# Binding side work to a place in each engine's queue, forming the setups' bias vectors another way, and another end for the last tile, in a four-layer graph network

## The chip, the cores and the metric

The kernel runs on one core of one Trainium2 chip. The metric is the device time of a run in microseconds (us). A core has a matrix engine (TensorE, PE in the profile), three engines for elementwise work (VectorE or DVE, ScalarE or ACT, GpSimd or POOL), and SyncE (SP), which here only issues DMAs. Each engine takes its instructions in the order of its own queue. PE reads its operands in SBUF and writes to PSUM; DVE and ACT read both; DMAs move data between DRAM and SBUF.

## The reference

128 graphs of 64 nodes with 512 features (8192 tokens, fp32) go through four layers. In each, `h = relu(layernorm(x))`, and then `x = x + layer(h)`:

```python
# layer 0 (Wqk gives q and k; the softmax runs over a graph's nodes)
agg = adj @ (k * mask);  w = mask * sum(q * agg, -1) / sqrt(512)
L0 = softmax(w, axis=1)[:, :, None] * (h @ Wv)
# layer 1
weight = adj * exp((h @ Wq.T + bq) @ (h @ Wk.T + bk).T)
L1 = (weight / weight.sum(2)) @ (h @ Wv.T + bv)
# layer 2: eight heads of 64, scores times 2*adj, softmax, then Wo and bo
# layer 3
Xw = h @ Wv + bv;  e = leaky_relu(Xw @ aw[:512] + (Xw @ aw[512:]).T + ab)
A = adj * exp(e);  A = A / A.sum(-1)
L3 = relu(h @ Wk[0] + bk[0] + A @ h @ Wk[1] + bk[1] + A @ A @ h @ Wk[2] + bk[2])
```

Layer 1's scores are formed without q and k: with `M = Wk Wq` folded once, `h_i M h_j + u . h_i + c . h_j + d` is the score, where u comes from Wq and bk, c from Wk and bq, and d = bq . bk. Layer 3's Xw is likewise never formed: `aw` is multiplied into Wv once (two vectors of 512, and two scalars from bv).

## The kernel before

**Tiling.** A block is 256 tokens (two tiles of 128, four graphs); there are 32 blocks. Layers 0 and 1 run over the blocks in pairs (`steps`: layer 0 of blocks b and b+1, then layer 1 of both), write x to DRAM, then layer 2 runs over all blocks, then layer 3. Each step holds `norm` (statistics on DVE, `rstd` on POOL at L171, `h` on ACT at L178), `transposed` (PE L189; the two halves of hT are copied out by DVE, L194, and ACT, L192), and products with 512x512 weights.

**Products.** The class `Product` multiplies 256x512 by 512x512 in seven products of half the size instead of eight (Strassen and Winograd's scheme). On the data side it needs the sums S1 to S4, which `sums` makes on POOL from hT (L213 to L216, S1 first, S3 last); on the weight's side it needs T1 to T4, four POOL instructions of 128x512 for each weight (L87, or L98 where they are postponed). Product 1 needs only hT, product 5 needs S1. The seven products are issued in three stages: `first` (L263), `second`, and `late`; `side_by_side` (L341) puts the stages of two products beside each other and runs the steps of other work, handed in as `between`, in the gaps. `keep_ab` (L275) copies partial results out of PSUM: p1 by ACT (L277), u2 by DVE (L278). `add_to` (L331) adds layer 2's output product to x.

**Postponed weight sums.** `later` puts a weight's four sums in a list, and `chore` (L95) takes a number from it. It is called between the stages of the steps. A scheduler decides where on POOL they go: it orders the instructions of each engine by when their operands are there, and may put them ahead of instructions that were written earlier. `tc.issue_after(i)` exists in the framework: instructions inside it are put behind instruction i on their engine, with no data passed and no wait added between engines.

**Start and setups.** L131 to L143 issue the first loads: x and adjT on SP, Wq's four parts on ACT's queue, Wk's four on SP, L0_Wv, then mcol (the node mask, L142) and the bias columns. `setup0` folds layer 0's weights and forms `msc` (L437) from mcol; layer 0 multiplies with it at L504 (agg) and forms the per-graph softmax (wd L511, sm_w L394, mn L522, att, x L538). `transpose_weight` writes a weight's transpose over the weight (PE L410, copies L414 on ACT and L416 on DVE). `folded` makes M (PE L424). `setup1` does the same for layer 1, and takes u, c and d from 24 matmuls: u (pu1, L453) from 16 of one column, c (pc1) from four of 128x512, whose stationary operand is bq laid out 128 times, and d (pd1, L468). In layer 1 the dot product with c is DVE's `hc` (L556). `setup3` multiplies Wv by the two columns of aw: for each, a column laid out 128 times is stationary (awr), and four 128x512 matmuls (pu, L740) give the vector on all partitions; pc (L751) does the scalars. It runs at layer 2's block 28.

**Layer 2** adds its output bias L2_bo to x on POOL (L977) at the start of each block. **The last tile** of layer 3 (`layer3_end`, L855) goes from PSUM through ACT (tz, L860), POOL (L862) and DVE (L863) to the output DMA.

Of the kernel before, what the change touches and what calls it, by code (L numbers as in the profile page):

```python
# [8 lines left out]
FP = mybir.dt.float32  # L9
# [16 lines left out]
def kernel(ctx: ExitStack, tc: tile.TileContext, a: dict, out: bass.AP):  # L26
# [68 lines left out]
    def chore(n: int = 1):  # L95
        for _ in range(min(n, len(chores))):
            w, (to, x, y) = chores.pop(0)
            nc.gpsimd.tensor_tensor(w[:, to], w[:, x], w[:, y], ALU.subtract)  # L98
# [36 lines left out]
    first = load_x(0, x_d[rows(0), :], 0), load_adjT(0, 0)  # L135
    f0 = [
# [4 lines left out]
    mcol = const.tile([P, n_tok // P], FP, tag="mcol", name="mcol")  # L141
    nc.sync.dma_start(mcol, a["maskcol"])  # L142
    b1q, b1k, b2q, b2k = (column(n) for n in ("L1_bq", "L1_bk", "L2_bq", "L2_bk"))  # L143
# [56 lines left out]

    def sums(hT, name: str, places=("S", "S")):
# [14 lines left out]
        nc.gpsimd.tensor_tensor(S3, A11, A21, ALU.subtract)  # L216
# [3 lines left out]
    class Product:  # L220
# [40 lines left out]
        def first(self, ops, w, beside: bool = False):  # L261

            self.early(ops, w, (1, 5) if beside else (1, 6))  # L263
            if not beside:
                self.keep_ab()
# [7 lines left out]
        def keep_ab(self):  # L273
# [4 lines left out]
            nc.vector.tensor_tensor(self.u2, self.b, self.p1, ALU.add)  # L278
# [51 lines left out]
        def add_to(self, x):  # L330
# [8 lines left out]
            nc.gpsimd.tensor_tensor(x[:, 1, F:], self.u3, x[:, 1, F:], ALU.add)  # L339

    def side_by_side(*parts, between=()):  # L341
# [18 lines left out]
        for acts in between:  # L360
            for act in acts:
                act()

# [76 lines left out]
    def setup1():  # L440


        qT, kT = (factor(a[f"L1_W{c}"], c, 1, nc.sync) for c in "qk")
        w1v = fetched("L1_Wv", 3, nc.sync)
        yield
        for w, c in zip((qT, kT), "qk"):
# [3 lines left out]
        pu = ps_sc.tile([P, K], FP, tag="sc", name="pu1")  # L450
        for i in range(K):
            for k in range(K):
                nc.tensor.matmul(  # L453
                    pu[:, i : i + 1], qT[:, k, i * P : (i + 1) * P], b1k[:, k : k + 1],
                    start=(k == 0), stop=(k == K - 1),
                )
        u = const.tile([P, K], FP, tag="u1", name="u1")
        nc.vector.tensor_copy(u, pu)
        bqr = med.tile([P, K, P], FP, tag="pT", name="bqr", bufs=3)
        nc.vector.tensor_copy(bqr, b1q.unsqueeze(2).to_broadcast([P, K, P]))  # L460
        pc = ps_mm.tile([P, D], FP, tag="mm", name="pc1")
        for k in range(K):
# [619 lines left out]
```

## Time and profile before

| | |
|---|---|
| median of three runs | 2736.61 us (2732.79 to 2737.43) |
| the profiled execution | 2732.14 us, its span 2730.2 us |
| PE busy | 2667.7 us (98%) |
| DVE busy | 1704.9 us (62%) |
| ACT busy | 945.8 us (35%) |
| POOL busy | 1291.3 us (47%) |
| DMA | 128.49 MB, mean 47 GB/s |

The span goes from the first to the last instruction; 1.94 us of the execution lie around it. The page has each engine's busy time, the span in 40 slices of some 68 us with tenths of busy time, the chain of work that ended last, and groups of like instructions. The trace answers further: which instruction an engine waited for and how long, single instructions in a stretch of time, and busy time in chosen windows. A line there names the program line (L248), the engine, the operation, and the tiles (out<-in); a number in square brackets is idle time of the engine just before it and what ended it. Two PE records stand for one fp32 matmul.

### The profile page before, as it was taken

Reading aid. Unit: us, or ns where it says so; the run is one execution under the profiler, and the core shown is the slowest. Engines: PE = TensorE matmul, PEld = TensorE weight load, DVE = VectorE, ACT = ScalarE, POOL = GpSimd, SP = SyncE. Lnnn points to the kernel's source line nnn. Section 1 sums busy time; section 2 is a strip of 40 time slices with the busy share of each in tenths; the row PEclk is TensorE's granted clock in tenths of the full one; section 3 lists DMA queues with packets and bytes.
Section 4 is the critical chain, followed back from the end, with each engine's and each line's share of the span. In section 5 each row is a group of like instructions: output and inputs, shape, how many; then the busy total and the mean of one; then the engine's idle time right before and its main releaser. Section 6 shows DMA issues by size and latency. Waiting matters only on the chain.

```text
span 2730.2 us, 52850 instructions
## 1 busy us (share of the span) xinstructions
PE 2667.7 (98%) x20808; PEld 2263.4 (83%) x20808; DVE 1704.9 (62%) x4386; ACT 945.8 (35%) x2292; POOL 1291.3 (47%) x1586
## 2 busy tenths in 40 slices
PE   8999999999999998999999999999999999999998
PEld 5788888888888887899999989999887777777776
DVE  3566666666666667555555555555567666666664
ACT  2333333433333332333333333333333333333332
POOL 3434343333334337456456456456454455554454
PEclk9999999999999999999999999999999999999999
DMA  4111100111111112111111111111111111111110
GB/s 144 49 39 44 34 34 34 34 35 42 42 34 46 37 44 94 37 36 38 52 36 38 51 36 38 51 37 37 48 64 50 50 51 55 55 55 50 50 49 32
DMA packets 102345, 128.49 MB, mean 47 GB/s; under 512 B 40528, under 2 KB 49744, under 8 KB 102096
## 3 DMA queue, kind: packets, MB, share of 16 engines
q1 hardware_dynamic: 101520, 124.07, 13.6%
q8 instruction: 163, 2.67, 0.4%
q10 hardware_dynamic: 576, 1.05, 0.1%
q14 instruction: 86, 0.70, 0.1%
HBM read 74.76 MB, written 50.33 MB: 46 GB/s over the span
## 4 chain that ended last, share of the span: by engine, by line
PE 71%; DVE 17%; POOL 4%; DMA 4%; ACT 2%; issue 2%; SPq 0%; ACTq 0%; POOLq 0%; DVEq 0%
PE ab_y L248 10%; PE dc_y L248 8%; PE ab_v L248 7%; PE dc_v L248 6%; PE ab_q L241 4%; PE ab_g L248 4%; PE ab_k L241 4%; PE ab_g L241 3%; PE po L386 3%; PE dc_k L241 3%; PE dc_q L241 3%; PE dc_g L248 2%; PE tr L189 2%; DMA x<-x 2%; PE dc_g L241 2%; DVE e L654 2%
## 5 line engine op out<-in xcount | busy, mean ns | idle before, releaser
L178 ACT ACTIVATE h<-x,nmr,rstd 128x512 f32<-128x512 f32 x256 | 198.0, 808 | 223.5 <-DVE nmr L173 188.9
L166 DVE BATCH_NORM_STATS2 stats<-x 128x6 f32<-128x512 f32 x256 | 166.1, 676 | 71.8 <-DMA x<-x 67.5
L171 POOL TENSOR_TENSOR rstd<-ve,neghalf 128x2 f32<-128x2 f32 x128 | 89.7, 700 | 254.6 <-DVE ve L169 254.4
L248 PE MATMUL ab_y<-L_Wk,hT 128*128 128x256 f32 x768 | 204.3, 388 | 3.3 <-DVE u_y L300 2.6
L248 PE MATMUL ab_v<-L_Wv,hT 128*128 128x256 f32 x768 | 201.9, 385 | 3.8 <-DVE u_v L278 2.9
L248 PE MATMUL dc_y<-L_Wk,S 128*128 128x256 f32 x768 | 199.8, 383 | 0.7
L248 PE MATMUL dc_v<-L_Wv,S 128*128 128x256 f32 x768 | 197.2, 379 | 1.7 <-DVE v L302 1.7
L248 PE MATMUL ab_y<-L_Wk,S 128*128 128x256 f32 x768 | 197.8, 380 | 0.0
L248 PE MATMUL ab_v<-L_Wv,S 128*128 128x256 f32 x768 | 197.1, 379 | 0.0
L248 PEld LDWEIGHTS ab_y<-L_Wk,hT 128*128 128x128 f32 x768 | 137.8, 190 | 70.1 <-issue 25.2
L248 PEld LDWEIGHTS dc_y<-L_Wk,S 128*128 128x128 f32 x768 | 144.6, 191 | 26.4 <-DVE y L850 6.9
L248 PEld LDWEIGHTS dc_v<-L_Wv,S 128*128 128x128 f32 x768 | 145.8, 190 | 21.9 <-DVE v L302 2.1
L248 PEld LDWEIGHTS ab_v<-L_Wv,S 128*128 128x128 f32 x768 | 146.1, 190 | 20.0
L862 POOL TENSOR_TENSOR tz<-tz,y 128x512 f32<-128x512 f32 x64 | 92.9, 1452 | 145.8 <-ACT tz L860 145.8
L248 PEld LDWEIGHTS ab_y<-L_Wk,S 128*128 128x128 f32 x768 | 143.8, 191 | 18.3
L248 PEld LDWEIGHTS ab_v<-L_Wv,hT 128*128 128x128 f32 x768 | 133.9, 191 | 19.1 <-DVE u_v L278 3.2
L323 POOL TENSOR_TENSOR qk<-u_q,p_q 128x256 f32<-128x256 f32 x32 | 23.3, 727 | 265.4 <-DVE u_q L307 265.4
L189 PE MATMUL tr<-ident,h 128*128 128x128 f32 x1024 | 135.8, 275 | 3.9 <-ACT h L178 2.2
L189 PEld LDWEIGHTS tr<-ident,h 128*128 128x128 f32 x1024 | 119.9, 142 | 15.7 <-ACT h L178 2.6
L278 DVE TENSOR_TENSOR u_v<-ab_v,p_v 128x256 f32<-128x256 f32 x96 | 40.6, 423 | 126.2 <-ACT p_v L277 126.2
L213 POOL TENSOR_TENSOR S<-hT 128x256 f32<-128x256 f32 x128 | 99.4, 776 | 35.5 <-ACT hT L192 33.1
L216 POOL TENSOR_TENSOR S<-hT 128x256 f32<-128x256 f32 x128 | 106.9, 835 | 1.6 <-DVE hT L194 0.4
(243 smaller groups left out, 6535.8 us busy)
## 6 DMA issues: line engine op xcount, KB each, us to landing
x<-x SPq DMA_DIRECT2D x128, 512.0 KB, 3.4
x<-in_x_dram SPq DMA_DIRECT2D x32, 512.0 KB, 3.5
out_dram<-x SPq DMA_DIRECT2D x31, 512.0 KB, 2.7
adjT<-in_adjT_dram SPq DMA_DIRECT2D x64, 64.0 KB, 2.0
adjq<-in_adj_dram SPq DMA_DIRECT2D x64, 64.0 KB, 2.3
L_Wk<-in_L_Wk_dram SPq DMA_DIRECT2D x16, 256.0 KB, 4.4
L_Wv<-in_L_Wv_dram SPq DMA_DIRECT2D x12, 256.0 KB, 4.6
q<-in_L_Wqk_dram ACTq DMA_DIRECT2D x4, 256.0 KB, 5.9
```

The lines of the kernel that those rows point to most:

```text
L166: nc.vector.bn_stats(stats[:, t, :], x[:, t, :])
L171: nc.gpsimd.tensor_tensor(rstd, ve, neghalf, ALU.pow)
L178: nc.scalar.activation(h, x[:, t, :], AF.Relu, bias=nmr[:, t : t + 1], scale=rstd[:, t : t + 1])
L189: nc.tensor.transpose(pt[:, k, :], h[:, k * P : (k + 1) * P], ident)
L213: nc.gpsimd.tensor_tensor(S1, A21, A22, ALU.add)
L216: nc.gpsimd.tensor_tensor(S3, A11, A21, ALU.subtract)
L241: nc.tensor.matmul(dst[:, m * P : (m + 1) * P], w[:, place, k, m * P : (m + 1) * P], left[:, k, :], start=key not in self.begun, stop=last ...
L248: nc.tensor.matmul(dst, left[:, k, :], w[:, place, k, :], start=key not in self.begun, stop=last and k == 1, skip_group_check=True,)
L278: nc.vector.tensor_tensor(self.u2, self.b, self.p1, ALU.add)
L386: nc.tensor.matmul(ps[t][half[g ^ t]], e[half[g], t, :], us[t][half[g]], start=True, stop=True)
L654: nc.vector.tensor_tensor(eh, eh, mx.unsqueeze(2).to_broadcast([P, TT * hq, N]), ALU.subtract)
L862: nc.gpsimd.tensor_tensor(tz[t], tz[t], y0[:, t, :], ALU.add)
```

## The change

It has seven parts.

- The load of mcol moves to the third place on SP, behind x and adjT.
- `setup1` no longer uses PE for u, c and d. L1_bq and L1_bk are loaded to all 128 partitions, and nine DVE instructions of 128x512 multiply and sum (`accum_out`): four for u, four for c, one for d. c is written to DRAM as a row of 512 and loaded back to all partitions.
- The postponed weight sums, layer 3's bias sums and layer 2's L2_bo additions are issued behind `behind[0]`, which is the last S3 of `sums` or the last POOL addition of `add_to`; in layer 2 at most one sum comes in a block, two at some places.
- `hc` is issued behind `u2` of the value product (`kept`).
- Where two products run side by side, `first` issues product 5 ahead of product 1.
- `setup3` makes aw's two columns stationary: four matmuls of 2x512 and four of 2x1. The result (2x513) goes to DRAM and back to all partitions.
- In the last block, tile 0 is finished by one DVE instruction from PSUM in place of ACT's scaling and POOL's addition.

```diff
@@ -93,9 +93,10 @@
         chores.extend((w, s) for s in sums_of_weights)
     def chore(n: int = 1):
-        for _ in range(min(n, len(chores))):
-            w, (to, x, y) = chores.pop(0)
-            nc.gpsimd.tensor_tensor(w[:, to], w[:, x], w[:, y], ALU.subtract)
+        with tc.issue_after(behind[0].ins):
+            for _ in range(min(n, len(chores))):
+                w, (to, x, y) = chores.pop(0)
+                nc.gpsimd.tensor_tensor(w[:, to], w[:, x], w[:, y], ALU.subtract)
     def fetched(name: str, place: int, queue):
         w = slot(place, name)
@@ -133,14 +134,14 @@
         return w
     first = load_x(0, x_d[rows(0), :], 0), load_adjT(0, 0)
+    mcol = const.tile([P, n_tok // P], FP, tag="mcol", name="mcol")
+    nc.sync.dma_start(mcol, a["maskcol"])
     f0 = [
         factor(a["L0_Wqk"][:, i * D : (i + 1) * D], c, 0, queue)
         for i, (c, queue) in enumerate((("q", nc.scalar), ("k", nc.sync)))
     ]
     w0v = fetched("L0_Wv", 1, nc.sync)
-    mcol = const.tile([P, n_tok // P], FP, tag="mcol", name="mcol")
-    nc.sync.dma_start(mcol, a["maskcol"])
-    b1q, b1k, b2q, b2k = (column(n) for n in ("L1_bq", "L1_bk", "L2_bq", "L2_bk"))
+    b2q, b2k = (column(n) for n in ("L2_bq", "L2_bk"))
     b1v = row("L1_bv")
@@ -213,7 +216,7 @@
         nc.gpsimd.tensor_tensor(S1, A21, A22, ALU.add)
         nc.gpsimd.tensor_tensor(S2, S1, A11, ALU.subtract)
         nc.gpsimd.tensor_tensor(S4, A12, S2, ALU.subtract)
-        nc.gpsimd.tensor_tensor(S3, A11, A21, ALU.subtract)
+        behind[0] = nc.gpsimd.tensor_tensor(S3, A11, A21, ALU.subtract)
         return {1: (A11, B11), 4: (A22, T4), 5: (S1, T1), 6: (S2, T2),
                 2: (A12, B21), 3: (S4, B22), 7: (S3, T3)}
@@ -260,7 +263,7 @@
         def first(self, ops, w, beside: bool = False):
-            self.early(ops, w, (1, 5) if beside else (1, 6))
+            self.early(ops, w, (5, 1) if beside else (1, 6))
             if not beside:
                 self.keep_ab()
@@ -275,7 +278,7 @@
             self.p1, self.u2 = self.temp("p1"), self.temp("u2")
             nc.scalar.copy(self.p1, self.a)
-            nc.vector.tensor_tensor(self.u2, self.b, self.p1, ALU.add)
+            self.kept = nc.vector.tensor_tensor(self.u2, self.b, self.p1, ALU.add)
         def keep_dc(self, bias=None):
@@ -336,7 +339,9 @@
             nc.vector.tensor_tensor(x[:, 0, F:], self.c, x[:, 0, F:], ALU.add)
             nc.vector.tensor_tensor(x[:, 0, :F], self.a, x[:, 0, :F], ALU.add)
             nc.vector.tensor_tensor(x[:, 1, :F], self.d, x[:, 1, :F], ALU.add)
-            nc.gpsimd.tensor_tensor(x[:, 1, F:], self.u3, x[:, 1, F:], ALU.add)
+            behind[0] = nc.gpsimd.tensor_tensor(
+                x[:, 1, F:], self.u3, x[:, 1, F:], ALU.add
+            )
     def side_by_side(*parts, between=()):
@@ -441,40 +447,41 @@
         qT, kT = (factor(a[f"L1_W{c}"], c, 1, nc.sync) for c in "qk")
+
+        bias = big.tile([P, 2, P, K], FP, tag="v", name="b1qk")
+        for i, n in enumerate(("L1_bq", "L1_bk")):
+            nc.sync.dma_start(
+                bias[:, i], a[n].rearrange("(o p) k -> o p k", o=1).to_broadcast([P, P, K])
+            )
         w1v = fetched("L1_Wv", 3, nc.sync)
         yield
+        u = const.tile([P, K], FP, tag="u1", name="u1")
+        cc = small.tile([P, K], FP, tag="cc", name="c1", bufs=1)
+        d = const.tile([P, 1], FP, tag="d1", name="d1")
+        for to, x, by in (
+            *((u[:, k : k + 1], qT[:, k, :], 1) for k in range(K)),
+            *((cc[:, k : k + 1], kT[:, k, :], 0) for k in range(K)),
+            (d, None, 1),
+        ):
+            junk = med.tile([P, P, K], FP, tag="agg", name="bias1", bufs=2)
+            nc.vector.scalar_tensor_tensor(
+                junk, bias[:, 0] if x is None else x.rearrange("q (k p) -> q p k", k=K), 1.0,
+                bias[:, by], ALU.mult, ALU.mult, accum_out=to,
+            )
+
+        crow = tc.dram_tile([1, D], FP, name="c1_row")
+        nc.sync.dma_start(crow.rearrange("o (k p) -> p (o k)", p=P), cc)
+        c1 = const.tile([P, 2, D + 1], FP, tag="u3", name="c1")[:, 0, :D]
+        nc.sync.dma_start(c1, crow.to_broadcast([P, D]))
         for w, c in zip((qT, kT), "qk"):
             transpose_weight(w, f"{c}1")
         m = folded(kT, qT, 1, 2)
         formed(m, nc.gpsimd)
-        pu = ps_sc.tile([P, K], FP, tag="sc", name="pu1")
-        for i in range(K):
-            for k in range(K):
-                nc.tensor.matmul(
-                    pu[:, i : i + 1], qT[:, k, i * P : (i + 1) * P], b1k[:, k : k + 1],
-                    start=(k == 0), stop=(k == K - 1),
-                )
-        u = const.tile([P, K], FP, tag="u1", name="u1")
-        nc.vector.tensor_copy(u, pu)
-        bqr = med.tile([P, K, P], FP, tag="pT", name="bqr", bufs=3)
-        nc.vector.tensor_copy(bqr, b1q.unsqueeze(2).to_broadcast([P, K, P]))
-        pc = ps_mm.tile([P, D], FP, tag="mm", name="pc1")
-        for k in range(K):
-            nc.tensor.matmul(pc, bqr[:, k, :], kT[:, k, :], start=(k == 0), stop=(k == K - 1))
-        c = const.tile([P, D], FP, tag="u30", name="c1")
-        nc.scalar.copy(c, pc)
-        pd = ps_sc.tile([P, 1], FP, tag="sc", name="pd1")
-        for k in range(K):
-            nc.tensor.matmul(
-                pd, bqr[:, k, :], b1k[:, k : k + 1], start=(k == 0), stop=(k == K - 1)
-            )
-        d = const.tile([P, 1], FP, tag="d1", name="d1")
-        nc.vector.tensor_copy(d, pd)
         formed(w1v, nc.gpsimd)
         w2 = [fetched(f"L2_W{c}", 4 + i, nc.sync) for i, c in enumerate("qk")]
         for w in w2:
             later(w)
-        yield m, u, c, d, w1v, w2
+        yield m, u, c1, d, w1v, w2
     def layer0(b: int, x, adjT, hs, hT, between):
@@ -553,9 +560,10 @@
         be = small.tile([P, TT], FP, tag="be", name=f"be_{b}")
         for t in range(TT):
             hc = med.tile([P, D], FP, tag="agg", name=f"hc_{b}_{t}", bufs=2)
-            nc.vector.scalar_tensor_tensor(
-                hc, hs[t], 1.0, c1, ALU.mult, ALU.mult, accum_out=be[:, t : t + 1]
-            )
+            with tc.issue_after(of_v.kept.ins):
+                nc.vector.scalar_tensor_tensor(
+                    hc, hs[t], 1.0, c1, ALU.mult, ALU.mult, accum_out=be[:, t : t + 1]
+                )
         nc.vector.tensor_scalar(be, be, d1, None, ALU.add)
         s = products(gT, hT, f"1_{b}")
         e = small.tile([P, TT, N], FP, tag="e", name=f"e1_{b}")
@@ -731,35 +739,31 @@
             )
             halves.append(w)
-        us = []
-        for s in range(2):
-            awr = med.tile([P, K, P], FP, tag="pT", name=f"awr{s}", bufs=3)
-            nc.vector.tensor_copy(awr, aw[:, :, s : s + 1].to_broadcast([P, K, P]))
-            pu = ps_sc.tile([P, D], FP, tag="sc", name=f"pu{s}")
-            for k in range(K):
-                nc.tensor.matmul(
-                    pu, awr[:, k, :], halves[k // 2][:, k % 2, :],
-                    start=(k == 0), stop=(k == K - 1),
-                )
-            u = const.tile([P, D], FP, tag=f"u3{s}", name=f"u3{s}")
-            nc.scalar.copy(u, pu)
-            us.append(u)
-        bvr = med.tile([P, K, P], FP, tag="pT", name="bvr", bufs=3)
-        nc.vector.tensor_copy(bvr, bv.unsqueeze(2).to_broadcast([P, K, P]))
-        pc = ps_sc.tile([P, 2], FP, tag="sc", name="pc3")
+        pu = ps_sc.tile([2, D], FP, tag="sc", name="pu3")
+        pc = ps_sc.tile([2, 1], FP, tag="sc", name="pc3")
         for k in range(K):
-            nc.tensor.matmul(pc, bvr[:, k, :], aw[:, k, :], start=(k == 0), stop=(k == K - 1))
-        cc = small.tile([P, 2], FP, tag="cc", name="cc", bufs=1)
-        nc.vector.tensor_copy(cc, pc)
+            for to, x in ((pu, halves[k // 2][:, k % 2, :]), (pc, bv[:, k : k + 1])):
+                nc.tensor.matmul(to, aw[:, k, :], x, start=(k == 0), stop=(k == K - 1))
+        us2 = big.tile([2, D + 1], FP, tag="v", name="us2")
+        nc.scalar.copy(us2[:, :D], pu)
+        nc.scalar.copy(us2[:, D:], pc)
+        urow = tc.dram_tile([2, D + 1], FP, name="u3_row")
+        nc.sync.dma_start(urow, us2)
+        uc = const.tile([P, 2, D + 1], FP, tag="u3", name="u3")
+        nc.sync.dma_start(
+            uc, urow.rearrange("(o s) d -> o s d", o=1).to_broadcast([P, 2, D + 1])
+        )
+        us = [uc[:, s, :D] for s in range(2)]
         c3 = const.tile([P, 1], FP, tag="c3", name="c3")
-        nc.vector.tensor_tensor(c3, cc[:, 0:1], cc[:, 1:2], ALU.add)
+        nc.vector.tensor_tensor(c3, uc[:, 0, D:], uc[:, 1, D:], ALU.add)
         nc.vector.tensor_tensor(c3, c3, ab, ALU.add)
         bs = const.tile([P, D], FP, tag="bs", name="bs")
         nc.sync.dma_start(bs, a["L3_bk"][0:1, :].to_broadcast([P, D]))
         for i in range(1, 3):
             bi = med.tile([P, D], FP, tag="agg", name=f"bk{i}", bufs=2)
             nc.sync.dma_start(bi, a["L3_bk"][i : i + 1, :].to_broadcast([P, D]))
-            nc.gpsimd.tensor_tensor(bs, bs, bi, ALU.add)
+            with tc.issue_after(behind[0].ins):
+                nc.gpsimd.tensor_tensor(bs, bs, bi, ALU.add)
         return us, c3, bs
     def layer3_norm(b: int, source):
@@ -857,9 +861,15 @@
         tz = [med.tile([P, D], FP, tag="pT", name=f"tz_{b}_{t}", bufs=3) for t in range(TT)]
         to, last = tokens(out[rows(b), :]), b + 1 == n_blk
         for t, out_at, at in neighbour_sums(po, al, [y[:, 0, t, :] for t in range(TT)]):
-            nc.scalar.activation(tz[t][out_at], po[t][at], AF.Copy, scale=r[at, t : t + 1])
-        for t in range(TT):
-            nc.gpsimd.tensor_tensor(tz[t], tz[t], y0[:, t, :], ALU.add)
+            if last and not t:
+                nc.vector.scalar_tensor_tensor(
+                    tz[t], po[t], r[:, t : t + 1], y0[:, t, :], ALU.mult, ALU.add
+                )
+            else:
+                nc.scalar.activation(tz[t][out_at], po[t][at], AF.Copy, scale=r[at, t : t + 1])
+        for t in range(TT):
+            if not last or t:
+                nc.gpsimd.tensor_tensor(tz[t], tz[t], y0[:, t, :], ALU.add)
             nc.vector.scalar_tensor_tensor(
                 x[:, t, :], tz[t], 0.0, x[:, t, :], ALU.max, ALU.add
             )
@@ -973,17 +983,19 @@
         later(w3[i])
     for b in range(n_blk):
         x = loaded2[b][0]
-        for t in range(TT):
-            nc.gpsimd.tensor_tensor(x[:, t, :], x[:, t, :], made2[1], ALU.add)
+        with tc.issue_after(behind[0].ins):
+            for t in range(TT):
+                nc.gpsimd.tensor_tensor(x[:, t, :], x[:, t, :], made2[1], ALU.add)
         stages = iter(())
         if b == n_blk - 2:
             stages = layer3_in(0, *normed3, made_in)
             next(stages)
         if b + 1 < n_blk:
-            qk, ops = layer2_in(b + 1, normed2[b + 1], [[chore], [chore]])
+            qk, ops = layer2_in(b + 1, normed2[b + 1], [[], [lambda: chore(1 if b else 2)]])
         else:
             parts = layer3_step(0, False)
             next(parts)
+            chore(2)
         if b == n_blk - 2:
             w3[0] = fetched("L3_Wk0", 4, nc.sync)
             later(w3[0])
@@ -1004,7 +1016,7 @@
         else:
             next(parts)
         side_by_side(part)
-        chore(4 if b == n_blk - 2 else 0)
+        chore(2 if b == n_blk - 2 else 0)
         nc.sync.dma_start(tokens(x2[b]), x)
         if b == n_blk - 4:
             made3 = setup3()

```

## The prediction

> **What bounds the kernel now.** I read the page's busy times first, then TensorE's waits, then windows and timelines around each wait.
>
> ```profile
> span 2730.2 us, 52850 instructions
> PE 2667.7 (98%) x20808; PEld 2263.4 (83%) x20808; DVE 1704.9 (62%) x4386; ACT 945.8 (35%) x2292; POOL 1291.3 (47%) x1586
> PE   8999999999999998999999999999999999999998
> ```
>
> TensorE (PE) is the bound: it idles 2730.2 − 2667.7 = 62.5 us. Only two things can shorten the run: that idle time (with the slow clock behind it), and matmuls left out. Slices are 68 us; the first and the sixteenth (1024–1092) are weak. The waits name the idle time:
>
> ```profile
> PE sm_w L394 <- DVE wd L511: 9.8, 15, 0.7
> PE ab_g L241 <- DVE u_g L278: 7.5, 16, 4.0
> PE ab_q L241 <- DVE hT L194: 6.0, 28, 0.4
> ...
> PE tw_k L410 <- DVE q L416: 3.9, 2, 3.3
> ...
> PE tr L189 <- ACT h L178: 2.2, 1, 2.2
> ```
>
> Columns: sum, times, longest. Fifteen waits of 0.65 us are one per even layer-1 block; 28 of 0.2 us are layer 2's; the rest are single stalls at changes of layer. The chain of waits shows two of them:
>
> ```profile
> 9.36 4.04 DMA mcol<-in_maskcol_dram
> ...
> 14.61 0.69 DVE q L416
> 15.34 3.36 PE tw_k L410 x15
> ...
> 84.42 1.28 POOL L_Wq L98
> 86.10 1.71 POOL L_Wk L98
> 87.88 3.71 POOL L_Wk L98 x3
> 91.59 0.67 POOL rstd L171
> 92.48 1.52 ACT h L178 x2
> ```
>
> **Start: +3.5 us.** mcol is issued on SP behind k's and L0_Wv's parts and lands at 13.40; DVE's msc waits for it and the q copies stand behind msc, so PE waits 3.33 us for tw_k. The transposes before it end at 11.9. With mcol third on SP and 0.4 us per issue ahead of it, it lands some 4 us sooner; the weights behind it on SP come one 0.34 us issue later. Gain between 0 (something else holds q) and 3.3 + 1 us of slow clock; I take 3.5. Chance of loss: L0_Wv's four sums, 5.05 us on POOL, now stand behind am_0 (0.58 us), nothing more.
>
> **setup1: +2.3 us.** Left out: 16 pu1 matmuls (4.30 us in the chain), pd1 (1.71), pc1 (4 of 128x512, 3.5). Added: two broadcast DMAs early on SP, a 2 KB round trip of c1 through DRAM, and nine 128x512 multiply-sums on DVE, which stand behind layer 0's two agg (they take their buffers) and ahead of the q/k copies (those overwrite what the nine read). Their row is hc: 0.66 us each beside an idle POOL, 1.20 beside a busy one. POOL was idle from 49.5 to 62, so 9 × 0.69 = 6.2 us, 51.6 to 57.8. Then q copies, tw_k, k copies, and pf_1 starts near 60.7 instead of 61.32 (+0.6); pc1's 3.4 us at 75.8 goes wholly. But PE now stands some 3 us before tw_k, which by the rows below halves its clock afterwards (−1.7). 0.6 + 3.4 − 1.7 = 2.3. Here a rule speaks against the change: eight of the nine read the weight with a step of 512 bytes. The Trainium skill's page "SBUF — State Buffer", section "🔬 SBUF: two separate sides", says that every access to a new 16-byte line costs extra, with no figure for VectorE. No row here shows such a read. By the quiet row I get +2.3; if the step doubles them (my estimate of the rule's worst), 8 × 0.6 = 4.8 more, −2.5. I take the hc row, as the same instruction, and keep −5 to +5. c1's round trip has over 40 us until hc reads it.
>
> **Weight sums (chores) behind S3 or the last x add: +5.5 us at 80–97.** Before, eight of them run at 80.62–91.59 ahead of rstd; PE waits 1.82 and 2.17 us:
>
> ```profile
> 88.32 1.13 PE L248 MATMUL ab_g<-fold,hT 128*128 128x256 f32 x4 [1.82 <-DVE u_g L278]
> ...
> 93.34 1.97 PE L189 MATMUL tr<-ident,h 128*128 128x128 f32 x8 [2.17 <-ACT h L178]
> 95.11 1.86 PE L248 MATMUL ab_v<-L_Wv,hT 128*128 128x256 f32 x4
> 96.81 1.03 PE L248 MATMUL ab_v<-L_Wv,S 128*128 128x256 f32 x4
> ```
>
> In the compiled order one sum at a time now follows S3, and rstd stands ahead. The two groups after the second wait take 1.97 + 1.86 where such groups take 1.04 + 1.03: 1.8 us of slow clock. The Trainium skill ("TensorE: Matmul & The Clock Gate", "HAM oscillation — how this bites in real kernels") asks for idle gaps over about 3.4 us before the clock falls: by that rule I would gain 1.82 + 2.17 = 4.0. The row is shorter than the rule's gap and slow all the same, so the row decides: 5.8, I take 5.5 (4.0 to 6).
>
> **hc behind u2_v: +11.5 us.**
>
> ```profile
> 406.80 1.20 DVE L556 SCALAR_TENSOR_TENSOR hc<-h,c 128x512 f32<-128x512 f32 x1
> ...
> 408.27 0.46 DVE L511 TENSOR_TENSOR wd<-eye,w 128x128 f32<-128x128 f32 x1
> ...
> 408.79 0.49 PE L394 MATMUL sm_w<-wd,ones_bd 128*128 128x128 f32 x2 [0.65 <-DVE wd L511]
> ```
>
> hc stands between agg and wd; PE waits for wd. Tied behind u2_v, it leaves that place, and wd is ready 1.2 us sooner: 15 × 0.65 = 9.8. x and mv follow sooner too, so the 0.24 us that ab_g waits 13 times (3.0) mostly goes: 9.8 + 1.7 = 11.5 (8 to 12.8). The 1.3 us of hc are late next before r L580 or u3_g and gT; those have 2 us until PE uses them.
>
> **1000–1100: +10.5 us.**
>
> ```profile
> 1000.00:1050.00 50.00, 44.66 (x291) 37.75 (x290) 38.16 (x89) 15.48 (x40) 31.79 (x32) 0.97 0.24 74
> 1050.00:1100.00 50.00, 43.13 (x411) 38.43 (x412) 33.15 (x71) 16.12 (x41) 33.11 (x34) 1.00 0.29 91
> ```
>
> The first number after the length is PE's: 12.2 us idle in 100. Here 16 sums (L_Wv, L_Wo, L3_Wk), two bs sums and two x adds stand in POOL's queue ahead of rstd and gv; the largest wait is 4.00 us, with 2.08 + 1.69 after it where 1.06 + 1.06 is usual (1.7 of clock). Now they are spread over blocks. All of it would be 11.6 + 1.7 = 13.3; some stays because the change of layer has its own chain: 10.5 (5 to 13.3).
>
> **Layer 2: −0.5 us.** Product 5 ahead of 1 lets PE start without hT's DVE half, so the 28 waits of 0.2 go; but the late ab_o then stands 0.1 us behind DVE's u_o, so I count 1 of 6. Against it, in blocks 0–7 the compiled order has one sum of 1.25 us on POOL among the last adds to x (between L333 and L335), and so ahead of the x2 store; a later load of x, and on DVE what stands behind that x, wait for the store (2.1 us once, at 1333.56). PE's ab_v has about 1 us of slack there, so I count 0.2 us each, 8 × 0.2 = −1.5 (together +5 to −6). L2_bo's x add (L977, 2.5 us per block) moves from ahead of its own block's sums behind the last x add of the block before, into a gap of POOL: nothing.
>
> **setup3: +4.5 us.** pu's 8 matmuls took 0.86 + 2.57 + 3.54 and pc 0.8, after a wait of 1.05 for w3vT: 8.8. Now four of 512 columns (two records each of 0.4375, pf's pace: 14.0 us for 32) are 3.5, and four tiny ones 0.8: 4.3. The new round trip through DRAM (4 KB out, 525 KB back) is bounded by x's own store and load: store issued 1327.02, read on DVE 1333.56, 6.5 us. It lands near 1952; PE needs it at 1972.6 (sm_i), DVE's c3 and hu queue from about 1951, and qk, u3_k and r stand behind them. Three us late cost nothing, ten cost 7: −3 to +5.
>
> **L3_Wk0's sums: +1.4** (the wait of ab_v at 1995; up to 5). **Last tile: +0.9**: ACT's tz halves 0.69 each and one POOL add of 1.26–1.66 leave the tail for one DVE step; tile 1's ACT half starts 0.7 sooner (0.5 to 1.1).
>
> **Sum.** 3.5 + 2.3 + 5.5 + 11.5 + 10.5 − 0.5 + 4.5 + 1.4 + 0.9 = 39.6. The profiled execution, 2732.1 (span 2730.2 and 1.9 around it), becomes 2692.5. The median of the runs lies 4.5 above it; carried over, 2697.
>
> **Rivals.** *The waits move*: nine slow DVE steps in setup1 (−3), layer 2's x stores late (−5), 1000–1100 half kept (5), setup3's round trip eats its gain (0): 3.5 − 3 + 5.5 + 9.8 + 5 − 5 + 0 + 1.4 + 0.9 = 18, or 2719. For it: POOL carries the same work, so each sum still delays something by 1.25 us; against it: POOL is only 47% busy. *S1 late, slower than before*: product 5 needs S1, which POOL writes from hT, where product 1 needs hT alone.
>
> ```profile
> 404.46 0.73 POOL L213 TENSOR_TENSOR S<-hT 128x256 f32<-128x256 f32 x1 [0.44 <-ACT hT L192]
> ...
> 406.19 1.05 PE L241 MATMUL ab_g<-hT,fold 128*128 128x128 f32 x8
> ```
>
> S1 ends 1.0 us before the first product starts. If a sum or an x add comes in front of it (1.25 us) in all 32 blocks of layers 0 to 2, PE loses up to 0.86 us (the cover of product 1) 96 times, 80 us: it decides from an average lateness of 0.45 us (43 us), and gives about 2745. Against it: sums stand behind S3, not before S1. *No effect of the ties*: if the sums still precede rstd, 5.5, 10.5 and 1.4 fall out: 2714. *More than summed*: 1000–1100 whole and 1 to 2 more at setup3, layer 2 and L3_Wk0 each: 2686.
>
> **How the numbers follow.** Likeliest case 0.60 (own range 2688–2708), waits move 0.18, more than summed 0.10, ties without effect 0.05, S1 late 0.07. The range leaves S1 and the far end of the best case out: 2682 to 2724. A measurement of this kernel tells 0.2% (5.5 us) from no change: faster 0.90, same 0.03, slower 0.07.
>
> **What would show it.** tw_k's wait gone near 15; nine L467 rows of 0.69 on DVE before q's copies; no sum rows between 80 and 92 and PE over 96% in 1000–1100; no wait of sm_w for wd; PE's first layer-2 product without a wait. Wrong if S L213 appears among PE's releasers, if DVE waits for u3's DMA beyond 1956, or if L467 rows take 1.2.

## The result, and the profile after

The changed kernel takes 2691.41 us (median of five runs, 2690.02 to 2695.23), the kernel before 2736.61 us (five runs, 2732.57 to 2737.64). The ratio is 0.9842, with a 95% interval of 0.9828 to 0.9857. The prediction was 2697, its range 2682 to 2724. The profiled execution took 2690.4 us, with a span of 2688.6 us: 41.6 us less than before. It lies 1 us below its median where the one before lay 4.5 below, so the medians differ by more (45.2) than the profiled executions.

The page's first lines of the kernel after: the span, the engines' busy time, and PE's busy tenths in 40 slices.

```profile
span 2688.6 us, 52721 instructions
...
PE 2646.6 (98%) x20752; PEld 2256.7 (84%) x20752; DVE 1682.3 (63%) x4398; ACT 942.7 (35%) x2290; POOL 1274.9 (47%) x1585
...
PE   8999999999999999999999999999999999999999
```

PE is busy 21.1 us less than before, and idles 42.0 us instead of 62.5. The weak slice at the first change of layer (the sixteenth) is gone. PE's waits after (sum, times, longest):

```profile
PE ab_o L251 <- DVE u_o L281: 6.9, 29, 0.5
PE tw_q L416 <- DMA q<-in_L_Wqk_dram: 5.3, 3, 4.6
PE ab_v L251 <- DVE stats L167: 3.7, 4, 1.5
PE s L642 <- POOL qk L326: 3.5, 1, 3.5
PE tw_k L416 <- DVE q L422: 3.3, 1, 3.3
PE ab_y L251 <- DVE u_y L303: 2.6, 1, 2.6
```

sm_w's fifteen waits of 0.65, ab_g's short ones (fifteen, where the prediction counted thirteen) and the single stalls at 88, 93 and 1035 are gone. New are ab_o's 29, which have taken the place of ab_q's 28, more waits of ab_v for stats in layer 2, and in setup1 those of tw_k and one of sm_w (1.46, behind the first multiply-sum on DVE).

To see where the 41.6 us came from, I took the start of each of the 128 transposes of hT (PE's `tr` rows, four for each block) in both traces, and subtracted. The lead of the changed kernel at such a landmark is all that it has gained so far. Such a lead comes from one profile of each kernel. In layers 0 and 1 it repeats to 0.1 us from pair to pair. At the start it does not: one of the kernels below, whose program up to the landmark at 40 is the changed kernel's, stands 1.9 us ahead of it there.

| stretch | lead at its end, us | gained in it | predicted |
|---|---|---|---|
| start (to the transpose at 40) | 3.87 | +3.9 | +3.5 |
| setup1 and the sums at 80–97 (to 97) | 12.40 | +8.5 | +2.3 and +5.5 |
| layers 0 and 1, 14 further pairs of blocks (to 940) | 33.11 | +20.7 | +11.5 |
| change to layer 2 (to 1032) | 43.59 | +10.5 | +10.5 |
| layer 2, blocks 1 to 28 | 36.42 | −7.2 | −0.5 |
| setup3 | 41.73 | +5.3 | +4.5 |
| change to layer 3, L3_Wk0 | 43.66 | +1.9 | +1.4 |
| layer 3 | 40.45 | −3.2 | 0 |
| end | 41.6 | +1.2 | +0.9 |

The sum was close (39.6 predicted), but by luck: two terms were far off, in opposite directions. Layers 0 and 1 gave 9 us more, layers 2 and 3 took 10 us more. The experiments are about these, and about the parts that the table can't tell apart.

### The profile page after: what moved, and what is told of

Its sections match the earlier page's. It is cut to its first block, busy times and chain, and to the rows that moved or that the text cites. A ratio compares the mean times of both kernels' runs of the same rounds, so it can differ in the third digit from the quotient of the medians.

```text
span 2688.6 us, 52721 instructions
## 1 busy us (share of the span) xinstructions
PE 2646.6 (98%) x20752; PEld 2256.7 (84%) x20752; DVE 1682.3 (63%) x4398; ACT 942.7 (35%) x2290; POOL 1274.9 (47%) x1585
## 4 chain that ended last, share of the span: by engine, by line
PE 77%; DVE 11%; DMA 5%; POOL 3%; ACT 2%; issue 2%; POOLq 0%; SPq 0%; ACTq 0%; DVEq 0%
PE ab_v L251 10%; PE ab_y L251 10%; PE dc_v L251 8%; PE dc_y L251 7%; PE ab_g L244 4%; PE ab_g L251 4%; DMA x<-x 4%; PE dc_g L244 3%; PE ab_q L244 3%; PE dc_g L251 3%; PE ab_k L244 3%; PE po L392 3%; PE tr L190 3%; PE dc_k L244 2%; PE dc_q L244 2%; DVE e L662 2%
## 5 line engine op out<-in xcount | busy, mean ns | idle before, releaser
L251 PE MATMUL dc_y<-L_Wk,S 128*128 128x256 f32 x768 | 193.8, 381 | 0.2 <-DVE u_y L851 0.2
```

Of the source, the lines that this page charges most:

```text
L251: nc.tensor.matmul(dst, left[:, k, :], w[:, place, k, :], start=key not in self.begun, stop=last and k == 1, skip_group_check=True,)
```

## The experiments

**hc alone, and the order of products alone.** Two kernels, each the kernel before with one part of the change. The first issues hc behind u2 of the value product:

```diff
...
+            with tc.issue_after(of_v.kept.ins):
                 nc.vector.scalar_tensor_tensor(hc, hs[t], 1.0, c1, ...)
```

> The kernel before with one part of the change: hc issued behind u2 of the value product. Theory A (a wait of PE costs more than the idle time listed, because PE also has to fill again after it): the 15 waits of sm_w (0.65 listed) and the waits of ab_g (0.24 listed) go, and each pair of blocks of layers 0 and 1 becomes 1.4 us shorter, 21 us in all: about 2715. Theory B (the prediction's own term: only the listed idle time goes): 0.77 us per pair, 11.5 us: about 2725, and the other 10 us of the changed kernel's layers 0 and 1 come from product 5 going ahead of product 1.

The second puts product 5 ahead of product 1:

```diff
-            self.early(ops, w, (1, 5) if beside else (1, 6))
+            self.early(ops, w, (5, 1) if beside else (1, 6))
```

> The kernel before with one part of the change: product 5 ahead of product 1 where two products stand side by side. Theory A: nothing in layers 0 and 1; in layer 2 the waits of ab_q for hT (0.2 each) turn into waits of ab_o for u_o of the same size; in layer 3 some 2 us are lost, since dc is released later than ab: 2736 to 2739, same or slightly slower. Theory B: about 10 us faster, 2726. Rival S1 late: slower by more than 10 us, with POOL's S among the releasers of PE.

Measured: hc alone 2713.71 us, ratio to before 0.9924 (0.9908 to 0.9941), 21.8 us faster than the median of the runs of before taken beside it. The order of products alone 2735.49, ratio 1.0001 (0.9993 to 1.0010). The landmarks agree: hc alone leads by 20.5 us at the end of layers 0 and 1, 1.48 for each pair of blocks, as the changed kernel does; the order of products moves nothing there (0.05 us over the 14 pairs). In these 14 pairs PE waits 28 times before, 12.4 us as listed, and not once with hc tied; 20.7 us are gained. So theory A holds as to the cost: the tie of hc gives all of it, and these waits cost more than their listed idle time. PE's timeline shows where the rest lies. Before, around one of the waits of sm_w:

```profile
407.08 1.06 PE L241 MATMUL dc_g<-S,fold 128*128 128x128 f32 x8
408.79 0.49 PE L394 MATMUL sm_w<-wd,ones_bd 128*128 128x128 f32 x2 [0.65 <-DVE wd L511]
409.12 1.06 PE L241 MATMUL ab_g<-S,fold 128*128 128x128 f32 x8
...
413.50 1.03 PE L248 MATMUL dc_v<-L_Wv,hT 128*128 128x256 f32 x4
414.76 1.16 PE L241 MATMUL ab_g<-hT,fold 128*128 128x128 f32 x8 [0.24 <-DVE u_g L278]
415.75 1.06 PE L241 MATMUL ab_g<-S,fold 128*128 128x128 f32 x8
```

After, the same stretch of the block:

```profile
388.68 1.06 PE L244 MATMUL ab_g<-hT,fold 128*128 128x128 f32 x8
389.57 0.39 PE L400 MATMUL sm_w<-wd,ones_bd 128*128 128x128 f32 x2
389.79 1.06 PE L244 MATMUL ab_g<-S,fold 128*128 128x128 f32 x8
...
394.17 1.03 PE L251 MATMUL dc_v<-L_Wv,hT 128*128 128x256 f32 x4
395.04 1.05 PE L244 MATMUL ab_g<-hT,fold 128*128 128x128 f32 x8
395.93 1.06 PE L244 MATMUL ab_g<-S,fold 128*128 128x128 f32 x8
```

Read the starts, not the idle time in brackets. A group of eight is followed after 0.89 us; its listed duration of 1.06 overlaps the next group by 0.17. With the wait, sm_w starts 1.71 after the group ahead of it (0.82 more), and the next group 0.33 after sm_w instead of 0.22 (0.11 more): the listed 0.65 costs 0.93. In the same way the listed 0.24 costs 1.26 − 0.87 + 0.99 − 0.89 = 0.49, and the transpose behind it 0.05 more. So each of these waits costs what is listed and about 0.26 us: some 0.16 because the group ahead no longer overlaps the next, and 0.1 because the one after that comes later too. 0.93 + 0.49 + 0.05 is 1.47 per pair, all but 0.01 of what the landmarks show. A slow clock is not the reason: the granted clock was 1.00 from 404 to 418. That PE's pipeline empties and fills again is a reading of these rows; no run shows the inside of PE.

**The order of products undone in the changed kernel.**

```diff
-            self.early(ops, w, (5, 1) if beside else (1, 6))
+            self.early(ops, w, (1, 5) if beside else (1, 6))
```

> The changed kernel with product 1 ahead of product 5 again, all else as changed. Theory A: within 3 us of the changed kernel, 2689 to 2692, layer 3 some 2 us shorter, layer 2 the same. Theory B: 10 us slower in layers 0 and 1, about 2701. If product 5 ahead of 1 causes layer 2's loss of 8 us, this comes back here: about 2683.

Measured: 2690.49, ratio to before 0.9834 (0.9820 to 0.9849), not told apart from the changed kernel's 0.9842 (0.9828 to 0.9857). In layers 0 and 1 the landmarks don't move (less than 0.1). In layer 2 ab_q's waits of 0.2 for hT and ab_o's of 0.2 for u_o change places, which the two kernels of the other direction show too. The order is worth nothing here that these runs could tell.

**Layer 2's sums behind the x additions.** The eight sums that stand one to a block at the start of layer 2 are called after the two additions of L2_bo instead of among the product's stages:

```diff
...
             for t in range(TT):
-                nc.gpsimd.tensor_tensor(x[:, t, :], x[:, t, :], made2[1], ALU.add)
+                behind[0] = nc.gpsimd.tensor_tensor(
+                    x[:, t, :], x[:, t, :], made2[1], ALU.add
+                )
+        if b:
+            chore()
...
-            ... [[], [lambda: chore(1 if b else 2)]])
+            ... [[], [lambda: chore(0 if b else 2)]])
```

> The changed kernel, but in layer 2's blocks 1 to 7 the one weight sum per block stands on POOL behind the two additions of L2_bo (POOL then idles over 6 us) instead of among the last additions to x. If the sum ahead of the x2 store causes layer 2's loss, 5 to 7 us come back: about 2685, and the waits of ab_v for stats or qk in blocks 1 to 7 are gone. If the order of products or the x additions cause it: the same as the changed kernel, 2691.

Measured: 2685.98, ratio 0.9818 (0.9803 to 0.9832); its interval still meets that of the changed kernel (0.9828 to 0.9857), so the landmarks have to decide. By them layer 2's first ten blocks are 6.1 us shorter than in the changed kernel, where they had lost 7.0, and later blocks give 2.5 us of it back. In the blocks with a sum nothing is lost any more (0.01 us or less against before), but for the first, where s waits as in the changed kernel. The edit also moves one of L3_Wk0's sums; the landmarks there stay as they were. So the sums are what these blocks lost by. The chain, in the changed kernel's block 4 (POOL, SP, DVE, PE):

```profile
1199.02 1.27 POOL L99 TENSOR_TENSOR L_Wk<-L_Wk 128x512 f32<-128x512 f32 x1
1200.25 0.72 POOL L338 TENSOR_TENSOR x<-u_o,x 128x256 f32<-128x256 f32 x1
1200.93 0.73 POOL L342 TENSOR_TENSOR x<-u_o,x 128x256 f32<-128x256 f32 x1
...
1201.68 0.37 SPq L1020 DMA_DIRECT2D x<-x  x1
1204.47 0.37 SPq L58 DMA_DIRECT2D x<-x  x1
...
1209.13 1.29 DVE L906 TENSOR_TENSOR x<-x,L_bv 128x512 f32<-128x512 f32 x2 [4.27 <-DMA x<-x]
...
1212.07 1.13 PE L251 MATMUL ab_v<-L_Wv,hT 128*128 128x256 f32 x4 [0.99 <-DVE stats L167]
```

The sum holds back the last additions to x, so the store (L1020), so the load into the buffer that it frees (L58), so DVE, where L906 stands ahead of the work that empties PE's PSUM. This is one of two blocks with a sum in which the load came latest (the other wait is 4.74, at 1090). In the others L906 waits 3.2 to 3.7 us, where it waited about 2.1 in most blocks before. With the sum behind the x additions, the same block:

```profile
1194.56 0.73 POOL L342 TENSOR_TENSOR x<-u_o,x 128x256 f32<-128x256 f32 x1
1195.24 2.50 POOL L988 TENSOR_TENSOR x<-x,L_bo 128x512 f32<-128x512 f32 x2
1197.70 1.26 POOL L99 TENSOR_TENSOR L_Wk<-L_Wk 128x512 f32<-128x512 f32 x1
1204.06 0.73 POOL L326 TENSOR_TENSOR qk<-u_q,p_q 128x256 f32<-128x256 f32 x1 [5.10 <-DVE u_q L310]
...
1201.70 1.29 DVE L906 TENSOR_TENSOR x<-x,L_bv 128x512 f32<-128x512 f32 x2 [1.98 <-DMA x<-x]
```

POOL has 5.1 us to spare behind the sum, and DVE waits 1.98 instead of 4.27. What remains is this load's small margin: waits of ab_v for stats come in a few blocks of each kernel, also of the kernel before (0.86 once, at 1630). They are the likely reason, not tested by itself, why gains in layer 2 come and go by 1 to 2 us from one profile to the next.

**setup1's biases as rows.** In the changed kernel's setup1, DVE's timeline:

```profile
47.02 1.02 DVE L467 SCALAR_TENSOR_TENSOR bias<-q,b1qk 128x512 f32<-128x512 f32 x1
...
53.94 1.03 DVE L467 SCALAR_TENSOR_TENSOR bias<-k,b1qk 128x512 f32<-128x512 f32 x1
...
54.88 0.69 DVE L467 SCALAR_TENSOR_TENSOR bias<-b1qk 128x512 f32<-128x512 f32 x1
55.50 1.29 DVE L422 COPY q<-tw_q 128x512 f32<-128x512 f32 x2
```

Eight of the nine take 1.03; only the ninth, which multiplies the two biases and reads no weight with a step, takes the 0.69 of the row that I had used. In the experiment the host lays bq and bk out as rows of 512, and both operands are read in order:

```diff
-                junk, bias[:, 0] if x is None else x.rearrange("q (k p) -> q p k", k=K), 1.0,
-                bias[:, by], ALU.mult, ALU.mult, accum_out=to,
+                junk.rearrange("p q k -> p (q k)"),
+                bias[:, 0].rearrange("p q k -> p (q k)") if x is None else x, 1.0,
+                bias[:, by].rearrange("p q k -> p (q k)"), ALU.mult, ALU.mult, accum_out=to,
...
-        "L1_bq": column(i["L1_gnn_Wq_b"]),
+        "L1_bq": i["L1_gnn_Wq_b"].reshape(1, D),
```

> The changed kernel with layer 1's two biases laid out as rows of 512, so that the nine multiply-sums of setup1 read both operands in order. If the step of 512 bytes made eight of them 1.03 us long (the ninth, without it, took 0.69), all take 0.69, the chain of nine ends 8 x 0.34 = 2.7 us sooner, tw_k's wait of 3.3 us shrinks by as much, and the run is 2.5 to 4 us faster: about 2688. If something else made them slow (the broadcast operand, the weight's slot), they stay at 1.03 and the time stays 2691.

DVE's timeline of this kernel, and below it of one that turns the reads round (the weight in order, the bias with a step of 16 bytes):

```profile
47.13 0.69 DVE L465 SCALAR_TENSOR_TENSOR bias<-q,b1qk 128x512 f32<-128x512 f32 x1
```

```profile
48.73 1.07 DVE L467 SCALAR_TENSOR_TENSOR bias<-q,b1qk 128x512 f32<-128x512 f32 x1
```

> The changed kernel with the multiply-sums turned round: the weight is read in order, the bias with a step of 16 bytes. If any step of 16 bytes or more costs a new line each time, the eight take 1.03 us as with 512 bytes; if only the large step costs, 0.69. The time says little: 2688 to 2692.

The edit of the second kernel:

```diff
-                junk, bias[:, 0] if x is None else x.rearrange("q (k p) -> q p k", k=K), 1.0,
-                bias[:, by], ALU.mult, ALU.mult, accum_out=to,
+                junk, ... x.rearrange("q (k p) -> q k p", k=K), 1.0,
+                ... bias[:, by].rearrange("q p k -> q k p"), ALU.mult, ALU.mult, accum_out=to,
```

In order 0.69, with a step of 512 bytes 1.03, with 16 bytes 1.07; POOL stands idle beside all three. So the step is the cause (or the two-dimensional read that goes with it in both kernels, which these runs don't part from it), and 16 bytes cost as much as 512. That agrees with the Trainium skill ("SBUF — State Buffer", "🔬 SBUF: two separate sides"), by which each access to a new 16-byte line pays; the size, half as much again, is these runs'. With rows, the landmark behind setup1 comes 3.2 us sooner. Of that the run shows little: 2689.46, ratio 0.9839 (0.9824 to 0.9854), since this profile loses 1.9 us again in layer 2's first blocks and 1.5 at the change to layer 3, at waits that change from kernel to kernel. The gain of the place is shown, that of the run is inconclusive. The kernel with the 16-byte step had one run, 2694.51.

**setup1 and setup3 back on PE.** Two kernels: the changed kernel with setup1 as before, and the changed kernel with setup3 as before (the removed lines of the change's diff put back, the added ones taken out).

> The changed kernel with setup1 as before: u, c and d by 24 matmuls on PE and no multiply-sums on DVE; all else as changed. From the landmarks the new setup1 gained some 1.5 to 2.5 us (3.4 of pc1, less 1 before the fold and 1 of slow clock): 2693 to 2694. If the nine steps on DVE cost as much as the matmuls did: 2691, no difference. If PE takes the matmuls into idle time it would have anyway: 2689.

> The changed kernel with setup3 as before (eight matmuls of 128x512 and four small ones on PE, no round trip through DRAM). If the new setup3 is worth the 4.5 us of the prediction: 2696. If it is worth all of the 5.3 us that the landmarks between blocks 28 and 30 show: 2697. If the round trip costs as much elsewhere as PE gains: 2691.

Measured: setup1 on PE 2693.70, ratio 0.9862 (0.9845 to 0.9878); by the landmarks 1.8 us are lost between 40 and 97, so the new setup1 is worth that. setup3 on PE 2697.51, ratio 0.9865 (0.9843 to 0.9888); by the landmarks 4.8 us are lost at setup3. Both intervals meet the changed kernel's, so it is the landmarks that bear out the prediction's terms (2.3 and 4.5), not the times. The round trip, issue of the store, issue of the load, and the first reader on DVE, in the changed kernel:

```profile
1908.87 0.31 SPq L751 DMA_DIRECT2D u_row<-us  x1
1911.01 0.36 SPq L753 DMA_DIRECT2D u<-u_row  x1
...
1915.42 0.15 DVE L758 TENSOR_TENSOR c<-u 128x1 f32<-128x1 f32 x1
```

It takes 6.55 us, where x's own round trip had given an estimate of 6.5, and the reader shows no wait.

**No ties.** The changed kernel, with the three ties behind `behind[0]` (weight sums, bias sums, x additions) taken out; the calls stay where the change put them.

```diff
-        with tc.issue_after(behind[0].ins):
+        with ExitStack():
... (the same at the two other ties)
```

> The changed kernel without the ties of the weight sums, the bias sums and the x additions: the scheduler places them freely, and in the compiled order L2_Wq's and L2_Wk's eight sums stand in a row ahead of rstd again, as do L2_Wv's and L2_Wo's and L3_Wk1's. If the ties are the cause of the gains at 80 to 97 (5.9) and at 1000 to 1100 (10.5) and of layer 2's loss (7 to 8), all three go: 5.9 + 10.5 + 1.4 - 7.5 = 10 us slower, about 2701, with waits of 1.8, 2.2 and 4.0 us on PE at the old places. If spreading the calls was enough: 2691 or, with layer 2's loss gone, 2684.

Measured: 2702.59, ratio 0.9882 (0.9867 to 0.9897). By the landmarks it loses 6.9 us to the changed kernel between 83 and 97, 9.5 at the change to layer 2 with layer 2's first block (where the changed kernel had gained 9.2), 1.6 at L3_Wk0, and gains 5.6 in the rest of layer 2. So spreading the calls does nothing without the ties. The wait is back, in another place than before and longer; PE's timeline:

```profile
92.02 2.08 PE L244 MATMUL dc_g<-S,fold 128*128 128x128 f32 x8 [4.50 <-POOL S L216]
```

**S1 late.** The rival that ends slower was tried directly: one more POOL addition of 128x512 ahead of S1 in every step of layers 0 and 1, once with product 5 first and once with product 1 first.

```diff
...
+        if name[0] in "01":
+            half_hT = hT[:, :, P : 2 * P].rearrange("p (a b) q -> p a b q", a=2)
+            nc.gpsimd.tensor_tensor(first_s[0], half_hT, half_hT, ALU.add)
         nc.gpsimd.tensor_tensor(S1, A21, A22, ALU.add)
```

> The changed kernel with one more POOL addition of 128x512 (its result is overwritten) ahead of S1 in every step of layers 0 and 1, 64 places, to test the rival S1 late. S1 then comes 1.3 us later, 2 where S3 goes ahead of it. By the rival, with 1.0 us of slack PE waits 0.3 to 1.0 us for S in each place and fills again (0.26): 0.5 to 1.2 us x 64 = 35 to 80 us slower than the changed kernel, 2725 to 2770, with POOL's S among PE's releasers. If the slack is larger than the 1.0 us read from the trace: under 2700.

> The same delay with product 1 ahead of product 5. Product 1 covers 0.87 us, so by the rival most of the wait goes: at most 0.1 to 0.4 us in each place, 2690 to 2720, and the difference to the kernel with product 5 first is what that order risks, up to 0.87 us x 64 = 55. If both are slowed alike, it is POOL's other work that is late, not S1.

Measured: product 5 first 2729.85, ratio 0.9984 (0.9977 to 0.9991), 38 us above the changed kernel; product 1 first 2706.51, ratio 0.9904 (0.9875 to 0.9933), 16 us above its own fellow without the delay. PE's waits, with product 5 first, and below with product 1 first:

```profile
PE dc_g L245 <- POOL S L217: 23.4, 16, 1.5
PE dc_g L252 <- POOL S L217: 7.8, 15, 0.5
```

```profile
PE dc_g L245 <- POOL S L217: 9.2, 16, 0.6
```

The mechanism is right: S becomes PE's releaser, and by the landmarks the order with product 5 first costs 20 us more in layers 0 and 1. It takes hold in half of the places (31 of 64); the others have more slack. The changed kernel itself shows no wait of a first product for S1, so the rival didn't come about.

These waits also test the price of a wait in another place, and it holds in only one of two. In the same 14 pairs of blocks they are listed with 27.8 us, and the landmarks show 31.9 lost, where 28 times 0.26 would have made it 35. From landmark to landmark, 1.46 ahead of L245's products (rows of 128x128) costs 1.73, and with product 1 first 0.57 costs 0.84: 0.27 more, as above. But 0.52 ahead of L252's products (128x256) costs 0.59, only 0.07 more. PE's timeline, in the changed kernel without this wait and below with it:

```profile
373.48 1.09 PE L392 MATMUL pa<-h,am 64*64 64x512 f32 x8
374.50 1.13 PE L251 MATMUL dc_g<-fold,S 128*128 128x256 f32 x4
375.46 1.03 PE L251 MATMUL ab_g<-fold,hT 128*128 128x256 f32 x4
```

```profile
386.55 1.09 PE L393 MATMUL pa<-h,am 64*64 64x512 f32 x8
388.16 1.13 PE L252 MATMUL dc_g<-fold,S 128*128 128x256 f32 x4 [0.53 <-POOL S L217]
389.13 1.03 PE L252 MATMUL ab_g<-fold,hT 128*128 128x256 f32 x4
```

Behind pa, whose matmuls have another shape, dc_g starts 1.02 later and ab_g 0.96 behind it even without a wait, where groups of dc_g and ab_g elsewhere follow after 0.86: 0.26 more for the two. My reading, not tested further, is that what a wait costs beyond its listed time is mostly lost at this place anyway.

**Three repairs together.** Layer 2's sums behind the x additions, biases as rows, and L2_Wo's last two sums behind the last part of block 1's qk (`store_T`'s POOL addition) instead of ahead of block 0's. For this last place the changed kernel's timeline of PE reads:

```profile
1044.13 0.48 PE L642 MATMUL s<-qk 64*64 64x64 f32 x16 [3.54 <-POOL qk L326]
1044.54 2.01 PE L251 MATMUL ab_v<-L_Wv,hT 128*128 128x256 f32 x4
```

```diff
-            ... [[], [lambda: chore(1 if b else 2)]])
+            ... [[], []])
+            if not b:
+                behind[0] = stored[0]
+                chore(2)
```

> Three repairs of the changed kernel together: layer 2's weight sums behind the x additions (5.4 us alone), biases as rows (2.5 to 4 expected), and L2_Wo's last two sums behind qk's last part of block 1 instead of ahead of qk of block 0, where PE waited 3.54 us and then ran at half clock (2 to 3.5 expected). If these are separate places they add up: about 2680. If the last one only moves the wait to the next block: about 2683.

Measured: 2679.64, ratio to before 0.9803 (0.9788 to 0.9818). Its interval lies below the changed kernel's (0.9828 to 0.9857): it beats the kernel before and the changed one, the latter by some 11 us. Against the changed kernel the landmarks show 3.0 in setup1, 7.7 in layer 2's first ten blocks and 2.4 in the first steps of layer 3, for which I have no cause; 1.9 of the 7.7 come in block 0, at L2_Wo's sums, where the wait of s fell from 3.5 to 2.0. From the kernel with layer 2's sums alone (0.9803 to 0.9832) the times don't part it.

## Why the prediction was right or wrong

The profiled execution came to 2690.4, 2.1 below the 2692.5 of the prediction's sum; this closeness is luck, since an error of +9 and one of −10 met. The other 3.5 us between 2697 and the median are the 4.5 that the prediction carried over from profile to median, and that turned out as 1.0. Most terms held. Those that failed by most are the price of hc's waits and the price of layer 2's sums.

**Start** (+3.5): right as far as it can be told, 3.9 where profiles differ by up to 1.9. msc is computed at 7.8 instead of 13.4, and tw_k follows without a wait.

**setup1** (+2.3): the sum is right (1.8), a row in it is wrong. The step "nine times 0.69" failed: I weighed the rule of the 16-byte lines against hc's row, and took the row because the instruction was the same; its operands weren't. Eight took 1.03, so the chain of nine ended 2.7 us later, and pf_1 began about 1 us later relative to the landmark ahead of it instead of 0.6 sooner. That the total came out was luck of the other terms. PE's slow clock behind the new wait was as expected:

```profile
58.00:64.00 6.00, 5.86 (x12) 2.55 (x11) 4.12 (x11) 1.61 (x6) 0.00 (x0) 0.70 0.00 0
```

The 0.70 is the granted clock of these 6 us, behind a wait of 3.3.

**Sums at 80–97** (+5.5): 6.7 by the landmarks (8.5 less setup1's 1.8), and 6.9 with the ties taken out. The row of two groups at half speed (the granted clock was 0.57 from 93 to 97 in the kernel before) was a better guide than the Trainium skill's gap of 3.4 us ("TensorE: Matmul & The Clock Gate", "HAM oscillation — how this bites in real kernels"), which would have given 4.0. The missing 1.2 us may be of the kind of hc's; that was not tested here.

**hc** (+11.5): the mechanism was right, its size was not: 20.7. The step that failed is the term "15 × 0.65 + 1.7". It counts listed idle time, and of ab_g's only a part; the 28 waits of 14 pairs are listed with 12.4 us, and each costs some 0.26 us beyond that, with 0.05 more per pair at the transpose.

**1000–1100** (+10.5): 10.5 up to the landmark at 1032 (1075 before). The stretch that was meant goes on for another landmark, and with it the gain is 9.2 (the ties alone 9.5, by the kernel without them): the stall of 3.54 at 1044 stands in place of three waits (1.54, 1.68 and 0.89) that the kernel before had there. PE is busy 94.5% of 1000 to 1100, where the prediction named over 96%.

**Layer 2** (−0.5): the mechanism was named (the sum ahead of the x2 store, the load, DVE's queue), its price was not: −7.2. The step "about 1 us of slack, so 0.2 us each" failed. The landmarks show 0.3 to 1.7 us lost in each of the first nine blocks: 1.3 in the first, with the stall at 1044; 1.7 and 1.3 in those with PE's waits for stats at 1093 and 1212, where the load itself was late on top of the sum; 0.3 to 0.7 in the six others. DVE's wait of 2.1 for the load, read there as coming once, stands in most blocks of layer 2 before. So even the mildest blocks lost more than 0.2, and the load's own variation was left out of the term. The "1 of 6" for the order of products was still too much: nothing.

**setup3, L3_Wk0, last tile** (+4.5, +1.4, +0.9): 5.3 (4.8 with setup3 undone), 1.9 and 1.2.

**Layer 3** (0): −3.2, of which 1.6 at its first step, where pc waits 2.29 for r instead of 1.03. The rest is spread with hardly a wait listed. The kernel with hc alone, whose layer 3 is that of before, loses 2.0 from its change of layer to its last transpose as well; so at least part of it is variation between executions. The order of products is not the cause: with it undone in the changed kernel, layer 3 loses 3.6. I don't claim another.

**The rivals.** "The waits move" described layer 2 and not the rest. "More than summed" came closest to the total (2686), for a reason that it didn't name. Ties without effect: refuted, they are worth 11 us. S1 late: no wait for S1 in the changed kernel; delayed on purpose, it costs 38 us in 31 of 64 places. Three sums of the prediction are slightly off, without effect on its result: 8 × 0.2 is 1.6, S1's 43 us on 2697 make 2740 and not 2745, and the additions named for "more than summed" end at 2688 to 2691.

## What to carry to other kernels

Price a wait of a busy PE by the starts of its neighbours, with and without the wait: here most short waits cost 0.26 us beyond their listed idle time, which doubled one of 0.24, and those at a place where PE's rows stood apart anyway cost 0.07. An instruction's row holds for its operands' order too: look for a row with the same step, and where there is none, take the rule. When side work is bound to a place in a queue, ask which store stands behind it and what load waits for the buffer: the best place was behind the last instruction that a store waits for, with idle time after it.

## What the runs showed that I had not expected

A DVE multiply-sum of 128x512 fp32 takes 0.69 us in order, 1.03 with one operand at a step of 512 bytes, and 1.07 at 16 bytes. A wait of 0.24 us on PE costs 0.49, but one of 0.52 behind matmuls of another shape only 0.59. And placing the same product one position earlier, which took away 28 waits of 0.2 us, brought 29 others of 0.2 us, so that the time stayed the same to within 0.1%.
